# Two banded layers on one core: in every fourth step GpSimd's group-norm pass for the next step moves ahead of the inverse square roots

## The chip, the cores and the metric

The kernel runs on one core of a Trainium2 chip. The metric is device time in microseconds, from one launch to its end; the median of three runs is 5162.48 us (5158.28 to 5162.59). The profile is one execution of 5160.82 us, whose instructions span 5158.9 us. The five engines are called as the profile calls them: PE (TensorE, matmuls and transposes), DVE (VectorE), ACT (ScalarE), POOL (GpSimd) and SP (SyncE, which here only issues transfers).

## The reference

An image `x` of 512 x 512 places with 64 channels goes twice through the same layer, each with its own weights:

```python
v = group_norm(x)                       # 32 groups of 2 channels, over the whole image
xn = layer_norm(v)                      # over the 64 channels of a place
left  = (xn @ Wl + bl) * mask * sigmoid(xn @ Wlg + blg)      # 64 -> 128
right = (xn @ Wr + br) * mask * sigmoid(xn @ Wrg + brg)
gate  = sigmoid(xn @ Wog + bog)
# each of 128 channels: out[i, k] = sum over |j - i| <= 4 of left[j, i] * right[j, k]
out = banded(left, right)
x = x + (layer_norm(out) * gate) @ Wo + bo
```

The mean and the variance of the group norm need the whole image, so layer 2 cannot begin its main work before layer 1 has ended. All arithmetic is float32.

## The kernel before

**Tiling.** A unit is a tile `z` of 128 x 8 x 64: 64 rows of the image, 8 columns, taken once from the left half and once from the right half of the image (two halves on 128 partitions). Sixteen units (`NU`) make a chunk of 128 columns; a layer has 9 row blocks of two chunks, that is 18 chunks or 288 units. Work runs in **steps** `t`, one unit per step; below, a step's place in its chunk is written t mod 16.

**What one unit goes through**, in four to twenty steps: `load` (two transfers of 128 KB, issued on SP two steps before use), `affine` (the group norm: `z * ga`, then `z + gb`, two POOL operations in place), `inner_stats` (layer-norm statistics on DVE, one step after `affine`), `solve` (the inverse square roots for some four units at once, every fourth step), `inner_norm` (`z - mean`, then `z * rs`, two POOL operations in place), `transposed` (four PE transposes, copied by ACT to `zT`), `right` (the projections on PE, a sigmoid on ACT to `sg`, the product on DVE into `RO`). When a chunk's `right` is complete, `mix` multiplies it with the banded `left` in the next chunk's steps, on PE (`banks<-RO,A`). Those matmuls fall in the places t mod 16 = 0 to 9 only; the places 10 to 15 have none.

**What one output goes through**: `out_stats` on DVE (`sto`), the same `solve`, `norm` on ACT (`on<-RO,nm,rs`), `gates` and `turned` on PE, a product on DVE (`ZH`), the projection back on PE, `biased` on POOL (adds the bias to the tile `XR` that holds the old image), a sum on DVE (`end`) and the store by SP. Outputs trail units by 30 steps. In places 10 and 11 `out_stats` is done for two outputs per step, in places 8 and 9 for none, else for one.

**Order.** Every engine gets its instructions in the order in which the step loop of `layer` writes them (the wrapper `en` keeps program order, which is why nearly all lines of the profile say L362). Within one step POOL gets:

```python
for u in affines.get(t, []):
    affine(u, en.vector if u.at < NU + 4 else en.gpsimd)   # z<-z,ga ; z<-z,gb
...
for u in inputs(t + 2):
    inner_norm(u)                                          # z<-z,sti ; z<-z,rs
...
    biased(outs[t], w, stats)                              # XR<-XR,pack (or fewer)
...
if t % 4 == 3:
    solve(w, us, os, st, so)    # DVE: 5 small; POOL: 10 rsqrt/rs, then rs and nm
```

`solve` at step T serves the units T+3 to T+6. The first of them meets `inner_norm` in step T+1, and its transposes stand in step T+2 on PE. The inverse roots and means of the outputs are first used by `norm` in step T+2. DVE's share of `solve` comes last in its step: it ends with `rs<-var`, the first guess of the root, on which POOL's `rsqrt<-rs` waits. `affines` is planned ahead by the list `count = [1, 1, 2, 1, 1, 1, 2, 1, 1, 1, 1, 0, 1, 1, 1, 0]`: so many units get `affine` in a step of that place, some 8 steps before they are transposed. Buffers: `z` has 12, the roots `rs` 3, the banks of PSUM (`bank`) 3 in layer 1 and 4 in layer 2.

Of the kernel before, what the change touches and what calls it, by code (L numbers as in the profile page):

```python
# [24 lines left out]
NU = JC // JU  # L25
# [22 lines left out]
def mid(v: bass.AP, n: int) -> bass.AP:  # L48

    p, c = v.shape  # L50
    return v.unsqueeze(1).broadcast_to([p, n, c])
# [28 lines left out]
def tile_two_banded_layers(  # L80
# [298 lines left out]
    def load(src: bass.AP, u: Unit):  # L379
        u.z = zp.tile([P, JU, D], F32, tag="z", name="z")  # L380
        if u.near is None:
            rows = slice(u.blk.s, u.blk.s + S)
            for e, j in enumerate((u.j, LH + u.j)):
                en.sync.dma_start(u.z[e * S : (e + 1) * S], src[rows, j : j + JU, :])
            return
        spans = [(0, u.near, u.near + JU)]
        if u.near + JU > NEAR * JQ:
            spans = [(o, u.near, u.near + JQ) for o in range(0, JU, JQ)]
        for o0, n0, n1 in spans:
            for o, r, k, m in runs(n0, n1):  # L390
                z = u.z[:, o0 + o : o0 + o + m, :].rearrange("q m c -> q (m c)")
                at, q0, q1 = r * (L + 1) + k - WIN, 0, P
                pieces = []

                if r == 0 and k < WIN:
                    q0, g = 1, min(m, WIN - k)
                    pieces = [(0, 0, g, 0), (0, g, m, at + g)]
                if r == JQ - 1 and k + m > WIN + 1:
                    q1, g = P - 1, max(0, WIN + 1 - k)
                    end = (P - 1) * JQ * (L + 1) + at  # L400
                    pieces = [(P - 1, 0, g, end), (P - 1, g, m, L * L - m)]
                en.sync.dma_start(
                    z[q0:q1],
                    strided(
                        src, (q0 * JQ * (L + 1) + at) * D, (JQ * (L + 1) * D, q1 - q0), (1, m * D)
                    ),
                )
                for q, g0, g1, a in pieces:
                    if g0 < g1:
                        en.sync.dma_start(  # L410
                            z[q : q + 1, g0 * D : g1 * D],
                            strided(src, a * D, (D, 1), (1, (g1 - g0) * D)),
                        )

    def affine(u: Unit, engine):

        engine.tensor_tensor(u.z, u.z, mid(ga, JU), ALU.mult)
        engine.tensor_tensor(u.z, u.z, mid(gb, JU), ALU.add)
# [171 lines left out]
    def recall(o: Out):  # L590
        o.t = ztg.tile([P, JU // 2, P], F32, tag="zg", name="zg")
        en.sync.dma_start(o.t, later[o.at])
# [81 lines left out]
    def layer(src: bass.AP, dst: bass.AP, w: dict, stats: bool, then=None):  # L674
        per = LH // JC
        n_chunks = len(blocks) * per
        LAG = NU + 14
        own = NU - JW // JU
        units, outs, lefts, mixes, looks, slabs = {}, {}, {}, {}, {}, {}
        free = NA * [NU - 2]  # L680
        for c in range(n_chunks):
            b, t0 = blocks[c // per], (c + 1) * NU
            for k in range(NU):
                t = c * NU + k
                units[t] = u = Unit(t, blk=b, j=c % per * JC + k * JU)
                j = k * JU if c % 2 == 0 else (JC + k * JU if k < own else JC - JW + (k - own) * JU)
                u.c = j

            for f in range(NU):
                o = outs[c * NU + LAG + f] = Out(  # L690
                    b, units[c * NU + (f + own) % NU], c % per * JC + f * JU
                )
                looks.setdefault(t0 + (8 + f if f > 3 else 10 + f // 2), []).append(o)

            step = [t0 + n for n, k in enumerate((2, 1, 2, 2, 1, 2, 1, 2, 2, 1)) for _ in range(k)]
            for n, t in enumerate(step):
                mixes.setdefault(t, []).append((c, n * HB))

            for h in range(H // HA):
                slabs.setdefault(free[-NA], []).append((c, h))  # L700
                free.append(step[(h + 1) * (HA // HB) - 1] + 1)
        for n in range(0, NEAR * JQ, JU):
            t = 3 + n // JU * 2
            lefts[t] = Unit(t, near=n)
        first_t, last_t = min(outs), max(outs)

        def inputs(t: int) -> list:
            return [d[t] for d in (units, lefts) if t in d]

        loads, affines, inners = {}, {}, {}
        count = [1, 1, 2, 1, 1, 1, 2, 1, 1, 1, 1, 0, 1, 1, 1, 0]
        ahead = {}
        done = -5 - NU
        for t in range(-7 - NU, n_chunks * NU):
            for _ in range(count[t % NU]):
                ahead[done + 7] = t
                done += 1
        for t in range(n_chunks * NU):  # L720
            for u in inputs(t):
                loads.setdefault(ahead[t] - 2, []).append(u)
                affines.setdefault(ahead[t], []).append(u)
                inners.setdefault(ahead[t] + 1, []).append((t, u))

        early = [u for t in sorted(loads) for u in loads[t] if u.near is None and u.at < 7]
        for u in early:
            load(src, u)
        yield
        A, sti, sto = {}, {}, None  # L730
        for t in range(min(loads), last_t + 3):
            if then and t == max(units) + 2:
                then()
            for u in loads.get(t, []):
                if u not in early:
                    load(src, u)
            if t + 2 in outs:
                recall(outs[t + 2])
            if t + 1 in outs:
                fetch(src, outs[t + 1], w, t + 1)  # L740
            for c, h in slabs.get(t, []):
                A[c, h] = take_left(c // per, h)

            for o in looks.get(t, []):
                if sto is None:
                    sto = sm.tile([P, NB // 2, 6], F32, tag="sto", name="sto"), []
                st, os = sto
                for k in range(JU // 2):
                    out_stats(o, st[:, len(os) * (JU // 2) :], k)
                os.append(o)  # L750
            for u in affines.get(t, []):
                affine(u, en.vector if u.at < NU + 4 else en.gpsimd)
            if t in outs:
                gates(outs[t], w)

            todo = []
            for at, u in inners.get(t, []):
                key = (at + 2) // 4
                if key not in sti:
                    sti[key] = sm.tile([P, 3 * NB // 4, 6], F32, tag="sti", name="sti", bufs=3), []  # L760
                st, us = sti[key]
                n = len(us) * (JU // 2)
                u.mean = st[:, n : n + JU // 2, 1::3]
                todo += [(u, st[:, n : n + JU // 2, :], k) for k in range(JU // 2)]
                us.append(u)
            for v in todo[: len(todo) // 2]:
                inner_stats(*v)
            if t in units:
                for q in range(0, JU, JQ):
                    right(units[t], q, w)  # L770
            if t in lefts:
                for q in range(0, min(JU, NEAR * JQ - lefts[t].near), JQ):
                    left(lefts[t], q, w)
            for u in inputs(t + 2):
                inner_norm(u)
            for u in inputs(t + 1):
                transposed(u)
            if t in outs:
                turned(outs[t], w)
                biased(outs[t], w, stats)  # L780
            for v in todo[len(todo) // 2 :]:
                inner_stats(*v)
            if t - 1 in outs:
                end(dst, outs[t - 1], w)
            if stats and t - 2 in outs:
                sums(outs[t - 2], t - 2 == first_t, t - 2 == last_t)
            if t % 4 == 3:
                st, us = sti.pop((t + 5) // 4, (None, []))
                so, os = sto or (None, [])
                sto = None  # L790
                if us or os:
                    solve(w, us, os, st, so)
            if t + 1 in outs:
                norm(outs[t + 1])
            for n, (c, h0) in enumerate(mixes.get(t, [])):
                mix(c, A[c, h0 // HA], h0, [True, n + 1 < len(mixes[t])])
# [129 lines left out]
```

## Time and profile before

| | |
|---|---|
| median of three runs | 5162.48 us (5158.28 to 5162.59) |
| profiled execution | 5160.82 us, span 5158.9 us |
| PE busy | 4536.4 us, 88% |
| POOL busy | 3821.0 us, 74% |
| ACT busy | 3793.4 us, 74% |
| DVE busy | 3656.7 us, 71% |
| mean DMA rate | 190 GB/s |
| granted PE clock, mean | 0.97 of full speed |
| POOL `z<-z,ga` and `z<-z,gb` | 536 each, 1280 and 1278 ns |
| POOL `z<-z,sti` and `z<-z,rs` | 586 each, 1064 and 1054 ns |

A busy share is an average over stages: the first 300 us collect the statistics of the input, both layers ramp up and down, and between is a steady part that repeats with each chunk. What the change is worth is read in the steady part, from what each engine waits for there. The steady part of layer 1 reaches in this profile from about 560 to 2470 us, that of layer 2 from about 3050 to 4880 us.

### The profile page before, as it was taken

The page shows a single profiled execution, that of the slowest core. Times are in us where ns is not written, and L with a number is a line of the kernel's source. Part 1 is how long each engine was busy: PE and PEld are TensorE (multiplying, and loading weights), DVE is VectorE, ACT ScalarE, POOL GpSimd, SP SyncE. Part 2 cuts the span into 40 slices and gives each one's busy share as a digit, 9 for nine tenths or more (in the row PEclk, how much of TensorE's full clock was granted, in tenths as well). Part 3 has the DMA queues.
Part 4 walks back from the last instruction along what each step waited for, and adds up shares of the span by engine and source line. Part 5 has one row for each costly group of instructions (what it writes and reads, how often), then busy time and mean ns, then how long its engine had stood idle before and what let it go on. Part 6 is the DMA issues. An engine that isn't in the chain of part 4 may idle for free.

```text
span 5158.9 us, 159784 instructions
## 1 busy us (share of the span) xinstructions
PE 4536.4 (88%) x60138; PEld 3756.4 (73%) x60138; DVE 3656.7 (71%) x9445; ACT 3793.4 (74%) x8328; POOL 3821.0 (74%) x4739
## 2 busy tenths in 40 slices
PE   1037999999999999999995599999999999999999
PEld 0025788888888888888873378888888887888886
DVE  6864677777777777777766467777777777777776
ACT  0013788888888888888884268888888888888888
POOL 0037888888888888888733588888888888888863
PEclk9988999999999999999998799999999999999999
DMA  7924666666666666666663457667677776667766
GB/s 318 387 62 127 176 190 191 190 192 190 193 190 190 190 191 190 191 192 192 187 169 108 105 172 200 196 197 200 194 200 199 199 199 195 194 199 200 200 186 172
DMA packets 905291, 981.45 MB, mean 190 GB/s; under 512 B 114210, under 2 KB 641608, under 8 KB 900168
## 3 DMA queue, kind: packets, MB, share of 16 engines
q1 hardware_dynamic: 897248, 948.49, 63.6%
q10 hardware_dynamic: 7272, 22.73, 1.1%
q8 instruction: 477, 7.82, 0.7%
q14 instruction: 294, 2.41, 0.2%
HBM read 658.42 MB, written 312.46 MB: 188 GB/s over the span
## 4 chain that ended last, share of the span: by engine, by line
PE 73%; POOL 9%; DMA 5%; DVE 5%; ACT 3%; issue 2%; SPq 2%; another core or an unknown queue 0%; ACTq 0%; POOLq 0%; DVEq 0%
PE banks L362 37%; PE bank L362 34%; POOL z L362 5%; POOL rsqrt L362 2%; DMA left_of<-nothing 2%; ACT on L362 2%; PE acc L362 2%; SPq L362 2%; DVE RO L362 1%; DVE ZH L362 1%; DMA gn_x<-in_x_dram 1%; POOL rs L362 1%; DMA z<-mid_x 1%; ACT gate L362 1%; DVE sti L362 0%
## 5 line engine op out<-in xcount | busy, mean ns | idle before, releaser
L362 ACT ACTIVATE on<-RO,nm,rs 128x128 f32<-128x128 f32 x4608 | 1878.3, 494 | 183.9 <-PE bank L362 178.3
L362 PE MATMUL banks<-pack,zT 64*128 64x256 f32 x9360 | 1219.7, 389 | 133.9 <-ACT zT L362 79.3
L362 PEld LDWEIGHTS banks<-pack,zT 64*128 64x128 f32 x9360 | 974.4, 193 | 413.6 <-issue 172.7
L362 PE MATMUL banks<-RO,A 64*64 64x128 f32 x18432 | 1154.6, 277 | 0.0
L362 PEld LDWEIGHTS banks<-RO,A 64*64 64x64 f32 x18432 | 1082.4, 183 | 26.7 <-issue 3.3
L362 ACT ACTIVATE sg<-banks 128x512 f32<-128x512 f32 (+1 forms) x1188 | 684.0, 589 | 323.4 <-PE banks L362 207.0
L362 DVE TENSOR_TENSOR RO<-banks,sg 128x512 f32<-128x512 f32 x1152 | 748.8, 682 | 231.0 <-ACT sg L362 230.1
L362 DVE COPY RO<-banks 128x512 f32<-128x512 f32 x360 | 249.0, 692 | 930.6 <-ACT RO L362 930.6
L362 DVE SCALAR_TENSOR_TENSOR ZH<-bank,pack,gate 128x448 f32<-128x448 f32 (+1 forms) x1152 | 742.6, 684 | 99.2 <-PE bank L362 61.4
L362 DVE BATCH_NORM_STATS2 sto<-RO 128x6 f32<-128x256 f32 x2304 | 797.8, 412 | 1.2
L362 POOL TENSOR_TENSOR z<-z,gb 128x512 f32<-128x512 f32 x536 | 685.2, 1278 | 42.0
L362 POOL TENSOR_TENSOR z<-z,ga 128x512 f32<-128x512 f32 x536 | 685.8, 1280 | 0.1
L362 PE MATMUL bank<-zg,pack 64*128 64x448 f32 (+1 forms) x2304 | 665.5, 597 | 18.6 <-DVE ZH L362 16.3
L362 PE MATMUL bank<-pack,ZH 128*64 128x64 f32 x18432 | 677.9, 228 | 3.0 <-ACT zT L362 0.5
L362 PEld LDWEIGHTS bank<-pack,ZH 128*64 128x64 f32 x18432 | 597.9, 140 | 103.6 <-ACT zT L362 76.7
L362 ACT ACTIVATE gate<-bank 128x448 f32<-128x448 f32 (+1 forms) x1152 | 566.5, 542 | 128.8 <-PE bank L362 127.9
L362 POOL TENSOR_TENSOR z<-z,rs 128x512 f32<-128x512 f32 x586 | 617.7, 1054 | 46.0
L362 PE MATMUL bank<-ident,on 128*128 128x128 f32 x4608 | 632.3, 279 | 14.7 <-ACT gate L362 12.1
L362 POOL TENSOR_TENSOR z<-z,sti 128x512 f32<-128x512 f32 x586 | 623.4, 1064 | 0.0
L362 ACT COPY RO<-banks 128x512 f32<-128x512 f32 x792 | 440.1, 585 | 225.7 <-PE banks L362 224.6
L362 DVE BATCH_NORM_STATS2 sti<-z 128x6 f32<-128x128 f32 x2344 | 549.0, 283 | 66.6 <-POOL z L362 66.6
L362 PEld LDWEIGHTS bank<-ident,on 128*128 128x128 f32 x4608 | 532.9, 144 | 73.9 <-ACT on L362 24.2
(137 smaller groups left out, 3725.3 us busy)
## 6 DMA issues: line engine op xcount, KB each, us to landing
later<-zT SPq DMA_DIRECT2D x576, 256.0 KB
A<-left_of SPq DMA_DIRECT2D x576, 256.0 KB
zg<-later SPq DMA_DIRECT2D x576, 256.0 KB
z<-in_x_dram SPq DMA_DIRECT2D x576, 128.0 KB
z<-mid_x SPq DMA_DIRECT2D x576, 128.0 KB
gn_x<-in_x_dram SPq DMA_DIRECT2D x16, 4096.0 KB
XR<-in_x_dram SPq DMA_DIRECT2D x448, 112.0 KB
mid_x<-XR SPq DMA_DIRECT2D x448, 112.0 KB
```

The source lines that it names most:

```text
L362: return lambda *a, **k: tc.keep_in_program_order(f(*a, **k))
```

## The change

In the steps with t mod 4 = 3 (from t = 19 on) the units due for `affine` in the next step are taken out of the plan and get it in this step, on POOL, just before `solve`. Nothing is added or left out.

```diff
-        A, sti, sto = {}, {}, None
+        A, sti, sto, then_affine = {}, {}, None, []
...
-            for u in affines.get(t, []):
+
+            for u in affines.pop(t, []):
                 affine(u, en.vector if u.at < NU + 4 else en.gpsimd)
+            if t % 4 == 3 and t > NU:
+                then_affine = affines.pop(t + 1, [])
             if t in outs:
                 gates(outs[t], w)
...
                 so, os = sto or (None, [])
                 sto = None
+                for u in then_affine:
+                    affine(u, en.gpsimd)
+                then_affine = []
                 if us or os:
                     solve(w, us, os, st, so)
```

## The prediction

> **What bounds the kernel now.** I read the page's chain first, because busy shares alone (PE 88%, the others 71 to 74%) do not say who waits.
>
> ```profile
> PE 73%; POOL 9%; DMA 5%; DVE 5%; ACT 3%; issue 2%; SPq 2%; another core or an unknown queue 0%; ACTq 0%; POOLq 0%; DVEq 0%
> ```
>
> PE carries the end, but 9% of the chain is POOL. Then I asked the table of waits who holds PE up, in the steady part of layer 1 (668 to 2470 us) and of layer 2 (3150 to 4880 us); columns: total us, times, longest.
>
> ```profile
> PE bank L362 <- POOL z L362: 38.3, 15, 2.6
> PE bank L362 <- DVE ZH L362: 8.9, 14, 0.6
> ...
> PE bank L362 <- POOL z L362: 53.7, 17, 3.5
> PE bank L362 <- DVE ZH L362: 4.0, 16, 0.3
> ```
>
> The reader is to see that PE is never out of work for long except for `z` from POOL, fifteen times per layer: once per chunk. The PE timeline gives the places: every 128.2 us in layer 1 (668.58 to 2463.27 us in 14 intervals), every 123.1 us in layer 2 (3152.59 to 4875.60). One of each follows, first on PE, then on POOL (start, duration, instruction, and in brackets the idle time before it).
>
> ```profile
> 1561.05 1.89 PE L362 MATMUL banks<-pack,zT 64*128 64x256 f32 x16
> 1565.49 0.66 PE L362 MATMUL bank<-ident,z 128*128 128x128 f32 x4 [2.55 <-POOL z L362]
> ```
>
> ```profile
> 1548.68 1.19 POOL L362 TENSOR_TENSOR XR<-XR,fewer 120x512 f32<-120x512 f32 x1 [2.04 <-PE bank L362]
> 1556.16 0.29 POOL L362 TENSOR_TENSOR rsqrt<-rs 128x64 f32<-128x64 f32 x1 [6.29 <-DVE rs L362]
> ...
> 1560.68 1.27 POOL L362 TENSOR_TENSOR z<-z,ga 128x512 f32<-128x512 f32 x1
> 1562.03 1.27 POOL L362 TENSOR_TENSOR z<-z,gb 128x512 f32<-128x512 f32 x1
> 1563.26 1.06 POOL L362 TENSOR_TENSOR z<-z,sti 128x512 f32<-128x512 f32 x1
> 1564.39 1.04 POOL L362 TENSOR_TENSOR z<-z,rs 128x512 f32<-128x512 f32 x1
> ```
>
> This is the solve at place 11. Places 10 to 15 have no mix matmuls, so PE's steps are short there; DVE has two outputs' statistics in each of places 10 and 11, so its share of the solve comes late. POOL idles 6.29 us for it, does the roots (4.5 us), then an `affine` that nobody needs yet (2.58 us, from 1560.68 to 1563.26), and only then the `inner_norm` that PE waits for.
>
> Last, the granted clock, in the stretches that follow stalls at 1436.85, 1565.49 and 3890.99 us, and a later one (the column before the DMA share is PEclk).
>
> ```profile
> 1436.80:1441.00 4.20, 4.15 (x50) 3.82 (x52) 1.77 (x4) 2.23 (x6) 4.12 (x4) 0.59 0.18 66
> 1565.40:1569.60 4.20, 4.11 (x68) 3.49 (x70) 2.98 (x8) 3.06 (x8) 4.12 (x5) 1.00 0.19 66
> 3890.90:3895.10 4.20, 4.11 (x45) 3.71 (x45) 1.77 (x4) 2.23 (x6) 4.12 (x5) 0.59 0.18 68
> 3895.10:3903.00 7.90, 7.90 (x89) 6.01 (x85) 7.34 (x20) 7.56 (x20) 7.67 (x8) 1.00 0.52 149
> ```
>
> A stall costs more than its idle time when PE resumes at about half clock: all fifteen of layer 2 (3.5 us idle) do, and eight of the fifteen of layer 1 (2.55 us idle).
>
> **What the Trainium skill says.** "TensorE: Matmul & The Clock Gate", section "What's actually happening": the clock falls to half after an idle window of about 3.4 us, the window runs freely. The trace agrees on layer 2 (3.51 us idle, 0.59 granted) but shows the drop after 2.55 us in half of layer 1's stalls too, where the page asks for a whole idle window; I use the trace. The same page, section "Architectural detail: the array is 16× 32×32, not 1× 128×128": GpSimd's queue is strictly first in, first out. The trace agrees: at 1549.9 us `z<-z,ga` could have run, and POOL idled in front of `rsqrt`. "GPSIMD Engine Reference", section "8. Key points": it contends with VectorE when the latter reads two inputs from SBUF. DVE's eight `sto` statistics took 2.71 us with POOL busy (at 1542.60) and 2.70 us with POOL idle (at 1548.98): no contention here.
>
> **The change part by part.**
>
> *What moves.* By the loop and its `count` list, 65 units per layer, 130 in all: 260 POOL operations pass in front of the 12 operations of their solve. No DVE, ACT, PE or SP instruction changes its place, and nothing is added: POOL's work is the same.
>
> *Place 11, layer 1.* POOL is free at 1549.87 us (1548.68 + 1.19). Its 2.58 us end by 1552.5 us, inside the idle 6.29 us, so `rsqrt` still starts at 1556.16. `inner_norm` then starts at 1560.7 and ends 2.58 us earlier, at 1562.86 instead of 1565.44 us. PE was free at 1565.49 - 2.55 = 1562.94 us. The whole stall goes: 15 x 2.55 = **38.3 us**. What is late next? POOL's own cadence in places 12 to 14 (two `affine` operations, two `inner_norm`, `XR`, 5.87 us a step, as between 1565.39 and 1571.27) moves forward as a whole by the same 2.58 us, so it does not take the gain back. DVE had 1.44 us idle for the same `z` and 1.60 us behind it; its product into `RO` will wait for ACT's sigmoid instead (ends 1563.84), some 0.6 us later than a plain shift, which an idle 1.14 us at 1571.74 takes up.
>
> *Clock, layer 1.* A stall at full clock gives an interval of 127.46 us (1309.39 to 1436.85), one at half clock 128.64 (1436.85 to 1565.49). Without the stall no window has reason to fall: 8 x 1.18 = **9.4 us**.
>
> *Place 11, layer 2.* The same arithmetic at 3890.99 us: POOL idle 6.34 us before `rsqrt`, the `affine` from 3886.19 to 3888.77. `z` is ready at 3888.37 instead of 3890.95, PE free at 3887.48: 0.93 us of stall remain, too short for a drop. Before, the half clock made that PE step 6.79 us (3890.99 to 3897.78) instead of 5.22, so PE fell behind POOL; after, POOL sets the next two steps (5.87 us each). Following both queues: `z` transposes at 3888.4, 3894.3, 3900.1, then 3905.4 us, against 3890.99, 3897.78, 3903.00, 3908.63 before. Gain 2.9 to 3.2 us a chunk; ACT's order (5.9 us a step) gives the same 3.2. I take 3.1: 15 x 3.1 = **46.5 us**. From below 2.58 (clock gives nothing), from above 4.2 (all of the 1.57 us too).
>
> *The ramps.* Steps before t = 19 keep the old order. The first solve at place 11 in each layer stalls PE by 5.31 us (at 541.56) and 4.12 us (at 3031.16), with POOL idle 5.04 and 4.02 us before it: 2.6 us each, part of the clock perhaps: **5.5 us**. After 4880 us no unit is left.
>
> *The other solves* (places 15, 3, 7). POOL idles 0.7 to 1.7, 2.2 to 2.7 and 3.9 us there in layer 1, and 0.7 to 2.4 us in layer 2 (steady part). Where that is less than 2.58 us, `rsqrt` starts up to 1.9 us later, but `inner_norm` never later: the sum of POOL's work ahead of it is the same. PE does not wait there, so I cost them at nothing. What covers the late roots is that `norm` uses them in step T+2, over a step of some 8 us away; without that cover up to 1.9 us per solve would fall on ACT.
>
> *The new wait.* `z<-z,ga` waits for its transfers, and behind it now stand `rsqrt`, the next `inner_norm` and PE. The loads are issued at the same place as before (1540.68 to 1541.80 us for the unit of 1560.68), some 8 us before POOL can reach them. In layer 2 the pair issued at 3866.55 is followed in SP's queue by the `XR` pair at 3868.33, and POOL used that `XR` at 3874.13 without waiting for a transfer; the moved `affine` starts at 3875.3. Landing is not shown by itself; from below the cost is nothing, from above what the third rival says. I take nothing.
>
> *Sum*: 38.3 + 9.4 + 46.5 + 5.5 = 99.7 us. The profiled execution has 5160.8 us, so 5061; the median of the runs shown lies 1.7 us above it: **5063 us**.
>
> **The rivals.**
>
> 1. *Half is given back.* After the stall ACT (5.9 us a step), POOL (5.87) and PE (5.2 to 5.9) run neck and neck in places 12 to 15. If ACT, whose idle 2.34 us before `zT` at 1566.18 disappears, holds PE by 1.3 us per chunk, and the clock still falls at times, some 30 x 1.3 + 10 us are lost: about 5112 us. For it: the small margins. Against it: ACT's copy is only some 0.2 us later than a plain shift, and PE needs it a step later.
> 2. *No change.* The `z` of the moved pass lands only when POOL's wait for DVE ends, so the idle time cannot be used: 5162 us. Against it: the `XR` evidence.
> 3. *Slower: the load holds the roots.* Place: the first operation of the moved `affine`, before the solve at place 11. It decides once `z` lands later than 1556.16 - 2.58 = 1553.6 us, 11.8 us after its issue; break-even is landing at 1556.1, 14.3 us after. At 2 us beyond that, PE waits 2 us longer in 32 chunks: 5162 + 64 = 5226 us. In the ramp POOL once waited 10.8 us for a `z` transfer; in the steady part never.
>
> That the reordering is not made is excluded by the loop: the units are popped from the plan and nothing else issues them.
>
> **How the numbers follow.** A measurement of this kernel can tell some 0.2%, 10 us, from no change. The main case gets 0.76 (its own range 5042 to 5083: all of the half-clock time gained, or 2.58 us per stall alone), the half gain 0.17, no change 0.02, slower 0.05. The range takes in the main case and most of the half gain: 5042 to 5104. Faster 0.93, same 0.02, slower 0.05.
>
> **What would show it.** After: the wait of PE for `z` from POOL near nothing in layer 1 and about 1 us in three places per chunk in layer 2; POOL's idle time before `rsqrt` at place 11 smaller by 2.6 us; `z<-z,gb` directly before `rsqrt<-rs`; a clock of 1.00 through both steady parts; chunks of about 125 and 120 us. I am wrong if `z<-z,ga` shows idle time ended by a transfer, if the wait before `zT` or `RO` grows into a wait of PE, or if chunks shorten by less than 2 us.

## The result, and the profile after

The changed kernel takes 5071.39 us (median; 5070.62 to 5074.14) beside 5161.35 us for the kernel before: a ratio of 0.9828, 95% interval 0.9811 to 0.9845. It is faster by 90 us where 99.7 were forecast. The profiled execution has 5074.14 us and a span of 5072.3 us, 86.6 less than before. One execution of the run e1 below took 14999.2 us at a granted clock of 0.35, and the ratios leave it out.

PE's waits in the steady part of layer 2 (3050 to 4860 us), then of layer 1 (640 to 2440 us); columns: total us, times, longest:

```profile
PE bank L362 <- POOL z L362: 31.6, 45, 1.0
PE banks L362 <- DVE RO L362: 14.1, 11, 1.4
PE bank L362 <- DVE ZH L362: 4.0, 15, 0.3
...
PE bank L362 <- DVE ZH L362: 9.5, 15, 0.6
PE banks L362 <- DVE RO L362: 1.4, 5, 0.3
```

In layer 1 the wait for `z` is gone. In layer 2 three short ones per chunk stand in place of each long one: 0.95, 0.59 and 0.58 us at 3098.00, 3103.88 and 3109.75 us. The prediction had 0.93 for the first, and its steps of 5.87 us on POOL beside 5.22 on PE leave 0.65 for each of the others. The second line is new: eleven times PE now waits some 1.28 us for `RO`. POOL at place 11 of layer 1 after the change (start, duration, instruction, idle time before it):

```profile
1397.09 1.18 POOL L362 TENSOR_TENSOR XR<-XR,fewer 120x512 f32<-120x512 f32 x1 [3.01 <-PE acc L362]
1398.24 1.28 POOL L362 TENSOR_TENSOR z<-z,ga 128x512 f32<-128x512 f32 x1
1399.59 1.27 POOL L362 TENSOR_TENSOR z<-z,gb 128x512 f32<-128x512 f32 x1
1406.21 0.29 POOL L362 TENSOR_TENSOR rsqrt<-rs 128x64 f32<-128x64 f32 x1 [5.34 <-DVE rs L362]
...
1410.74 1.05 POOL L362 TENSOR_TENSOR z<-z,sti 128x512 f32<-128x512 f32 x1
```

The pass fills a part of the idle time, 5.34 us of it are left, and `inner_norm` follows the roots at once. The granted clock (the column before the DMA share) over 34 us of layer 1 and over the 4.2 us after a wait of layer 2:

```profile
1406.00:1440.00 34.00, 33.72 (x475) 27.70 (x471) 28.29 (x68) 30.84 (x71) 31.36 (x46) 1.00 0.68 204
...
3098.00:3102.20 4.20, 4.20 (x56) 3.53 (x58) 4.20 (x10) 3.50 (x9) 4.12 (x4) 1.00 0.53 177
```

It is full in both, as everywhere in the steady parts. A chunk takes 125.1 us in layer 1 and 120.8 in layer 2 (means of 14), beside 128.2 and 123.1 before.

**Where the missing microseconds went.** The profile has a number that the prediction had not asked about: DVE is busy for 3732.8 us instead of 3656.7, with the same 9445 instructions. The groups of DVE show which: the solve's small operations `var<-sti`, `var<-sto,pack`, `var<-var` and `nm<-sto` went from means of 249, 193, 181 and 176 ns to 396, 314, 399 and 280 ns. One solve at place 15 of layer 2, first DVE, then POOL, then PE at the start of the mix:

```profile
3113.48 0.69 DVE L362 TENSOR_SCALAR var<-sti 128x32 f32<-128x32 f32 x1
3114.09 1.32 DVE L362 SCALAR_TENSOR_TENSOR var<-sto,pack 128x32 f32<-128x32 f32 x1
3115.44 0.18 DVE L362 TENSOR_SCALAR var<-var 128x32 f32<-128x32 f32 x1
3115.53 1.27 DVE L362 TENSOR_SCALAR nm<-sto 128x32 f32<-128x32 f32 x1
3116.72 0.18 DVE L362 TENSOR_SCALAR rs<-var 128x64 int32<-128x64 int32 x1
```

```profile
3112.93 1.19 POOL L362 TENSOR_TENSOR XR<-XR,pack 120x512 f32<-120x512 f32 x1
3114.07 1.28 POOL L362 TENSOR_TENSOR z<-z,ga 128x512 f32<-128x512 f32 x1
3115.44 1.32 POOL L362 TENSOR_TENSOR z<-z,gb 128x512 f32<-128x512 f32 x1
```

```profile
3118.87 0.39 PE L362 MATMUL banks<-RO,A 64*64 64x128 f32 x2 [1.28 <-DVE RO L362]
```

Read the ends: `var<-sti` ends at 3114.17 and POOL's `XR` at 3114.12; `var<-sto,pack` at 3115.41 and `z<-z,ga` at 3115.35; `nm<-sto` at 3116.80 and `z<-z,gb` at 3116.76. Each long DVE operation ends just after the POOL operation beside it. This is the rule and not one case: from 560 us on, 121 of these operations (with `rs<-var`) took over 0.45 us in the changed kernel, 18 in the kernel before, and every one of them ended 0.03 to 0.06 us after a POOL instruction. The five in the solve shown take 3.4 us, from 3113.48 to 3116.90; behind them in DVE's order, without idle time, stand the last products into `RO`, which the mix needs.

In the kernel before, a solve at place 15 of layer 2 takes 1.2 us on DVE (3168.07 to 3169.29). First DVE, then POOL:

```profile
3168.07 0.65 DVE L362 TENSOR_SCALAR var<-sti 128x32 f32<-128x32 f32 x1
3168.65 0.19 DVE L362 SCALAR_TENSOR_TENSOR var<-sto,pack 128x32 f32<-128x32 f32 x1
...
3168.97 0.17 DVE L362 TENSOR_SCALAR nm<-sto 128x32 f32<-128x32 f32 x1
```

```profile
3167.51 1.18 POOL L362 TENSOR_TENSOR XR<-XR,pack 120x512 f32<-120x512 f32 x1
3169.37 0.29 POOL L362 TENSOR_TENSOR rsqrt<-rs 128x64 f32<-128x64 f32 x1 [0.68 <-DVE rs L362]
```

POOL stands still beside all but the first, because it waits for the last of these very operations. The first shows that the warning was in the trace before the change: `var<-sti` runs beside `XR`, takes 0.65 us where it takes 0.18 beside an idle POOL (3090.43 us in the changed kernel), and ends with `XR`. Place 11 escapes: there POOL has finished the pass long before. In layer 1 the five operations grow too, from 54.5 to 85.8 us in all from 640 to 2440 us, but PE waits for `RO` for 1.4 us only; what covers them there, and in the four chunks of layer 2 without the wait, was not followed.

### The profile page after: what moved, and what is told of

It reads as the page before. It is cut to its first block, busy times and chain, and to the rows that moved or that the text cites. A ratio compares the mean times of both kernels' runs of the same rounds, so it can differ in the third digit from the quotient of the medians.

```text
span 5072.3 us, 159784 instructions
## 1 busy us (share of the span) xinstructions
PE 4496.1 (89%) x60138; PEld 3714.8 (73%) x60138; DVE 3732.8 (74%) x9445; ACT 3793.8 (75%) x8328; POOL 3826.9 (75%) x4739
## 4 chain that ended last, share of the span: by engine, by line
PE 72%; POOL 9%; DMA 6%; DVE 4%; ACT 3%; issue 2%; SPq 2%; another core or an unknown queue 0%; ACTq 0%; POOLq 0%; DVEq 0%
PE banks L362 38%; PE bank L362 32%; POOL z L362 6%; ACT on L362 2%; DMA left_of<-nothing 2%; PE acc L362 2%; SPq L362 2%; DVE RO L362 1%; POOL XR L362 1%; DMA gn_x<-in_x_dram 1%; POOL rsqrt L362 1%; DVE ZH L362 1%; DMA XR<-mid_x 1%; DVE sto L362 1%; ACT gate L362 1%
## 5 line engine op out<-in xcount | busy, mean ns | idle before, releaser
L362 DVE SCALAR_TENSOR_TENSOR ZH<-bank,pack,gate 128x448 f32<-128x448 f32 (+1 forms) x1152 | 740.0, 682 | 37.6 <-ACT gate L362 36.3
L362 PE MATMUL bank<-pack,ZH 128*64 128x64 f32 x18432 | 663.5, 225 | 2.8 <-ACT zT L362 0.3
L362 PEld LDWEIGHTS bank<-pack,ZH 128*64 128x64 f32 x18432 | 584.0, 138 | 100.3 <-ACT zT L362 83.2
L362 PE MATMUL bank<-ident,on 128*128 128x128 f32 x4608 | 616.6, 274 | 14.7 <-ACT gate L362 12.1
L362 PEld LDWEIGHTS bank<-ident,on 128*128 128x128 f32 x4608 | 519.7, 141 | 74.0 <-ACT on L362 24.3
L362 POOL TENSOR_TENSOR XR<-XR,pack 120x512 f32<-120x512 f32 (+1 forms) x352 | 418.4, 1189 | 192.4 <-DMA XR<-mid_x 90.4
```

The costliest lines, as they stand in the source:

```text
L362: return lambda *a, **k: tc.keep_in_program_order(f(*a, **k))
```

## The experiments

| run | median us | ratio to before, 95% interval |
|---|---|---|
| changed kernel | 5071.39 | 0.9828 (0.9811 to 0.9845) |
| e1: place 11 only | 5058.77 | 0.9803 (0.9783 to 0.9822) |
| e2: places 15, 3, 7 only | 5175.02 | 1.0025 (1.0015 to 1.0035) |
| e3: moved pass in quarters | 5062.90 | 0.9833 (0.9796 to 0.9871) |
| e4: half of the pass, place 11 | 5105.23 | 0.9895 (0.9880 to 0.9910) |
| e5: e1 with a late load | 5080.30 | 0.9844 (0.9827 to 0.9860) |
| e6: e1, output scales later | 5049.78 | 0.9787 (0.9772 to 0.9802) |
| e7: e1, two units ahead | 5045.86 | 0.9781 (0.9766 to 0.9795) |
| e8: e6 and e7 together | 5037.10 | 0.9763 (0.9748 to 0.9777) |

**e1: only the solve at place 11 keeps the pass ahead of it.**

```diff
-            if t % 4 == 3 and t > NU:
+            if t % NU == 11 and t > NU:
                 then_affine = affines.pop(t + 1, [])
```

> The pass is moved ahead of the solve at place 11 only; at places 15, 3 and 7 it stays where it was. Theory (the gain is all from place 11, and the moved pass at the other places runs beside DVE's small operations of the solve and lengthens them, which holds PE up at place 0 of 11 chunks of layer 2 by some 1.28 us): PE's waits for RO in front of the mix go, chunks of layer 2 shorten from 120.9 to about 120.0 us, DVE's small operations (var, nm) return to the means of the kernel before (181 to 249 ns instead of 280 to 399), about 5058 us (5054 to 5063). Rival (the moves at the other three places carry part of the gain): slower than the changed kernel's 5071, up to 5100 us.

Measured 5058.77 us, and in the steady part of layer 2 PE has only these waits left:

```profile
PE bank L362 <- POOL z L362: 31.4, 45, 1.0
PE bank L362 <- DVE ZH L362: 4.4, 18, 0.3
```

The wait for `RO` is gone, chunks of layer 2 take 119.9 us, and the three middle operations are back at 189, 181 and 175 ns (`var<-sti` is still at 337: at place 15 it starts while POOL's `XR` runs). So one place out of four carries the whole gain of 103 us, and the other three cost 12.6 (the difference of the two medians).

**e2: the other three places, without place 11.**

```diff
-            if t % 4 == 3 and t > NU:
+            if t % 4 == 3 and t % NU != 11 and t > NU:
```

> The pass is moved ahead of the solve at places 15, 3 and 7 only; at place 11 it stays behind the roots. Theory: PE's fifteen stalls per layer for z return at 2.55 and 3.5 us with their half clock; DVE's small operations are as long as in the changed kernel (means of 280 to 399 ns), but the stall at place 11 gives DVE the slack that hides it: about 5162 us (5155 to 5180). Rival (the gain comes from GpSimd's earlier work at any solve): three quarters of it remain, about 5094 us.

5175.02 us, slower than before by a quarter of a per cent, with an interval clear of 1. In layer 2:

```profile
PE bank L362 <- POOL z L362: 49.2, 14, 3.5
PE banks L362 <- DVE RO L362: 6.8, 10, 0.7
```

The stalls are back in full and the wait for `RO` stays, at 0.7 us instead of 1.3. I had expected DVE's operations as long as in the changed kernel and the stall's slack to hide them. Neither came out: the means of `var<-sto,pack` and `nm<-sto` are 228 and 189 ns, near those of the kernel before, and in the solve behind the wait at 3424.93 the five take 2.6 us (3420.40 to 3422.97) instead of 3.4. There `var<-sti` starts 0.3 us after `z<-z,ga` and not 0.6 us before it, and one operation fewer is held to the end of a POOL instruction. The time lies 13 us above the 5162 that I had put first; the waits for `RO` are 7.7 us of that (both layers), the rest was not followed. The rival of 5094 us is out.

**e3: each moved operation in four pieces of 128 elements.**

```diff
                 for u in then_affine:
-                    affine(u, en.gpsimd)
+                    for k in range(4):
+                        v = u.z[:, 2 * k : 2 * k + 2, :]
+                        en.gpsimd.tensor_tensor(v, v, mid(ga, 2), ALU.mult)
+                    ...                            # the same with gb, ALU.add
```

> As the changed kernel, but each moved operation of 512 elements per partition is issued as four of 128 (eight instead of two instructions per unit). Theory (a small DVE operation waits until the GpSimd instruction in progress has ended): no small DVE operation is longer than some 0.6 us, the means of var and nm fall towards 250 ns, PE's wait of 1.28 us at place 0 falls below 0.6 us or goes, about 5062 us (5055 to 5070); place 11 is not hurt, since GpSimd has over 5 us idle there. Rival (the two engines share bandwidth, whatever the length of an instruction): the small operations stay as long as they are and the wait of 1.28 us stays, 5071 us or more.

5062.90 us (three of the four executions took 5061.41 to 5063.80 us, one 5104.45, which makes the interval wide and stays unexplained). The same solve at place 15, on DVE:

```profile
3112.69 0.69 DVE L362 TENSOR_SCALAR var<-sti 128x32 f32<-128x32 f32 x1
3113.30 0.19 DVE L362 SCALAR_TENSOR_TENSOR var<-sto,pack 128x32 f32<-128x32 f32 x1
3113.52 0.31 DVE L362 TENSOR_SCALAR var<-var 128x32 f32<-128x32 f32 x1
3113.75 0.17 DVE L362 TENSOR_SCALAR nm<-sto 128x32 f32<-128x32 f32 x1
3113.86 0.42 DVE L362 TENSOR_SCALAR rs<-var 128x64 int32<-128x64 int32 x1
```

Behind `XR`, which is still one long operation, nothing is longer than 0.42 us here (0.51 is the most that `var<-sto,pack` and `nm<-sto` reach in the run), and PE's waits for `RO` fall from 14.1 to 2.1 us, although POOL has more to do (1.78 us for the four `ga` pieces instead of 1.28). That the length of one POOL instruction bounds the delay is so supported. The expected means were missed: they are 347, 315, 275 and 295 ns, `rs<-var` has grown as well, and the total of the five groups is the 240 us of the changed kernel, against 153 before. The waits are shorter but more solves have them; what the two engines share, and by which rule, these runs do not settle.

**e4: only `z * ga` ahead, at place 11.** It asks what the length of the stall is worth.

```diff
                 for u in then_affine:
-                    affine(u, en.gpsimd)
+                    en.gpsimd.tensor_tensor(u.z, u.z, mid(ga, JU), ALU.mult)
+                halves = then_affine               # z + gb: first on POOL in the next step
```

> At place 11 only, and only the first of the pass's two operations (z times ga) is moved ahead of the solve; the second stays behind the roots. PE's stall should be 1.29 us shorter: about 1.27 us in layer 1, 2.2 us in layer 2. Theory (a long stall also costs half-clock time): no half clock follows the 1.27 us, so layer 1 gains 15 x 1.29 + 9.4 = 28.8 us; layer 2 gains 15 x 1.3 = 19.5 us if the half clock stays, 30 us if it goes; with 2.6 us in the ramps 5100 to 5111 us in all, chunks of layer 1 all equally long. Rival (the clock has no part): 33 x 1.29 = 42 us gained, 5119 us, with the half clock still in every second chunk of layer 1.

5105.23 us. The stalls are 1.20 us in layer 1 and 2.17 us in layer 2. Clock after two stalls of layer 2 and one of layer 1:

```profile
3122.90:3127.10 4.20, 4.19 (x56) 3.53 (x58) 3.06 (x8) 3.14 (x8) 4.12 (x4) 1.00 0.27 82
3243.90:3248.10 4.20, 4.16 (x46) 3.76 (x46) 1.78 (x5) 1.87 (x5) 4.12 (x4) 0.59 0.36 115
793.70:797.90 4.20, 4.15 (x68) 3.53 (x70) 3.61 (x9) 3.10 (x8) 4.12 (x4) 1.00 0.28 90
```

No stall of 1.20 us is followed by half clock, nine of the fifteen of 2.17 us are. Chunks of layer 1 take 126.15 us (128.19 before): 2.0 us shorter for a stall that is 1.35 us shorter. The half clock is a price of its own; the rival's 5119 us lies outside the run's 5101.28 to 5107.52.

The length of the stall alone does not decide, though: 2.17 us are followed by half clock in nine of fifteen cases, 2.55 us before the change in eight of fifteen. And one stall of 3.51 us, the first in the steady part of layer 2 of the kernel before, is followed by full clock:

```profile
3152.50:3156.70 4.20, 4.11 (x56) 3.45 (x58) 2.98 (x8) 3.06 (x8) 4.12 (x5) 1.00 0.17 64
```

In the steady parts the granted clock changes only at times that are whole multiples of 3.413 us apart: in the kernel before half clock begins at 1437.34 and at 1693.34 us, 75 such intervals later. I cut PE's 90 long waits for `z` in the steady parts of three traces (before, e2, e4) at these times. Where at least 2.02 us of the wait lie inside one interval, half clock follows at that interval's end (55 cases); where at most 1.97 us do, it does not (35 cases). The wait that ends at 1436.85 lies whole in one interval. The one that ends at 1565.49 is cut into 0.69 and 1.85 us, and the clock stays full. A chunk of layer 1 is 37.6 intervals long, so the cut falls elsewhere in each chunk. The stall of the line above is cut into twice 1.75 us.

**e5: the load of the moved unit one step later, to bring about the prediction's slower rival.**

```diff
-                loads.setdefault(ahead[t] - 2, []).append(u)
+                late = ahead[t] % NU == 12 and ahead[t] > NU
+                loads.setdefault(ahead[t] - 2 + late, []).append(u)
```

> As e1_only11, but the transfers of the unit that is passed ahead at place 11 are issued one step later, at the start of place 11 instead of place 10, some 6 us before DVE's part of the solve ends instead of some 14 us. This is the prediction's slower rival, made to happen. Theory: an XR transfer landed within some 4.6 us of its issue here, so z lands some 1.5 to 1.9 us too late for the pass to be over when rsqrt could start; rsqrt waits that long in 32 chunks: about 5110 us (5080 to 5140), with a wait of z<-z,ga for a DMA in the trace. Rival (transfers land in 2 us): as e1_only11, 5058 us.

5080.30 us, 21.5 more than e1, at the low edge of what was expected. POOL:

```profile
3100.54 1.27 POOL L362 TENSOR_TENSOR z<-z,ga 128x512 f32<-128x512 f32 x1 [4.30 <-DMA z<-mid_x]
3101.89 1.28 POOL L362 TENSOR_TENSOR z<-z,gb 128x512 f32<-128x512 f32 x1
3103.84 0.29 POOL L362 TENSOR_TENSOR rsqrt<-rs 128x64 f32<-128x64 f32 x1 [0.67 <-DVE rs L362]
```

The pass does wait for its transfer, but the roots do not wait for the pass: `z` had landed within 3.5 us of its issue at 3097.09, the pass ends at 3103.17, and `rsqrt` then still idles 0.67 us for DVE. In all 32 such solves the pass ends before DVE's `rs<-var`. So the slower rival was not made to happen. What costs here is again DVE beside POOL:

```profile
3102.47 0.74 DVE L362 TENSOR_SCALAR var<-sti 128x32 f32<-128x32 f32 x1
```

It ends at 3103.21, just after `z<-z,gb`, and the five operations take 1.3 us; over the 32 solves their mean is 1.32 us, and 0.73 in e1. That is 0.6 us in each, which would make 19 of the 21.5 us. With the load where the change left it, a step or some 9 us earlier, the rival had no chance.

**e6: the solve's last two POOL operations (`rs`, `nm` for outputs) behind the next `inner_norm`.**

```diff
-            en.gpsimd.tensor_tensor(ro, ro, w["m"][:, js], ALU.mult)
-            en.gpsimd.tensor_tensor(nm, nm, ro, ALU.mult)
+            def out_scales(): ...                  # these two, called after
+            rest.append(out_scales)                # inner_norm of step T+1
```

> As e1_only11, but the solve's last two GpSimd operations (rs and nm for the outputs, 0.6 us) stand behind the next step's inner_norm instead of ahead of it. Theory (behind the roots GpSimd's own cadence sets PE's steps at places 12 to 14 of layer 2): the first wait of PE for z falls from 0.95 to 0.35 us, the second grows by 0.6 us, nothing is gained: 5058 us (5055 to 5062). Rival (only the chain up to the first z counts): 15 x 0.6 = 9 us less, 5049 us.

5049.78 us, 9.0 less than e1: the rival's number. The trace does not follow the rival, though. PE at places 12 to 14 of one chunk of layer 2:

```profile
3091.28 0.66 PE L362 MATMUL bank<-ident,z 128*128 128x128 f32 x4 [0.30 <-POOL z L362]
...
3097.69 0.65 PE L362 MATMUL bank<-ident,z 128*128 128x128 f32 x4 [1.12 <-POOL z L362]
...
3103.56 0.66 PE L362 MATMUL bank<-ident,z 128*128 128x128 f32 x4 [0.58 <-POOL z L362]
```

The first wait shrank and the second grew, as my theory had it, and chunks shortened by 0.19 us in layer 2 and 0.13 in layer 1, some 5 us in all. The other 4 us lie outside the steady parts, 2.4 of them in the ramp of layer 2 (from its first transposes to its first chunk, 234.8 us in e1 and 232.4 here). Why that ramp shortened is open.

**e7: at place 11 the pass for two units.**

```diff
-                loads.setdefault(ahead[t] - 2, []).append(u)
+                early_load = ahead[t] % NU == 13 and ahead[t] > NU
+                loads.setdefault(ahead[t] - 2 - early_load, []).append(u)
...
-                then_affine = affines.pop(t + 1, [])
+                then_affine = affines.pop(t + 1, []) + affines.pop(t + 2, [])
```

> As e1_only11, but at place 11 the pass is done ahead of the solve for the units of both places 12 and 13 (the second one's transfers are issued a step earlier). GpSimd has 4.5 us idle there, so the roots start on time; places 12 and 13 then have no pass to do. Theory (ACT, 5.87 us a step, is as full as GpSimd): PE's second and third waits for z in layer 2 (0.59 and 0.58 us) go, but ACT's sigmoid and so RO come no earlier, and PE waits about 0.9 us for RO at place 0: 5055 us (5052 to 5059). Rival (GpSimd alone held these steps): 15 x 1.17 = 17 us less, 5041 us.

5045.86 us, 12.9 less than e1, between the two and nearer to the rival. The second and third wait for `z` are gone, and no wait of PE for `RO` over 0.3 us has come in their place. ACT shows why my theory failed:

```profile
3095.86 3.25 ACT L362 ACTIVATE on<-RO,nm,rs 128x128 f32<-128x128 f32 x8 [0.35 <-PE bank L362]
...
3101.29 3.24 ACT L362 ACTIVATE on<-RO,nm,rs 128x128 f32<-128x128 f32 x8
...
3106.71 3.27 ACT L362 ACTIVATE on<-RO,nm,rs 128x128 f32<-128x128 f32 x8
```

ACT's 5.87 us a step had held a pause of 0.35 us for PE's transposes. With PE earlier the pause goes, and ACT runs at 5.42 us a step (3101.29 to 3106.71): the limit lay there, not at 5.87. Chunks of layer 2 take 119.3 us.

**e8: e6 and e7 together.**

```diff
+            rest.append(out_scales)                # as in e6
...
+                then_affine = affines.pop(t + 1, []) + affines.pop(t + 2, [])   # as in e7
```

> e6_defer and e7_two11 together, for the version that may beat both kernels. Theory (ACT holds places 12 to 15): as e7_two11, 5055 us (5050 to 5059). Rival (GpSimd alone held them): 15 x 1.77 = 27 us less than e1_only11, 5032 us.

5037.10 us, nearer to the rival again. In layer 2:

```profile
PE bank L362 <- DVE ZH L362: 4.5, 17, 0.3
PE bank L362 <- POOL z L362: 4.3, 15, 0.3
```

This version beats both kernels: 123 us less than before (5159.97 us, measured with it), 34 less than the change. It reads the same data and does the same operations, but only place 11 has the pass moved, for two units, with two small operations of the solve moved behind the next `inner_norm`.

## Why the prediction was right, and which term was off

The sum was 99.7 us against the profiled execution, and its span fell by 86.6. The mechanism held, and the shortfall has one cause, which e1 takes away. The stretches between the same instructions in the two traces split that:

- *Ramps*, 5.5 us predicted. The first `z` stall of layer 1 moves from 541.56 to 538.55 us (3.0), the ramp of layer 2 (from its first transposes, 2795.53 and 2745.80, to 3031.16 and 2979.14) shortens by 2.3: 5.3. Right.
- *Layer 1 with its clock*, 38.3 + 9.4 = 47.7 us. From that stall to the statistics between the layers (2766.92 and 2717.15) it is 2225.4 before and 2178.6 after: 46.8. Right, and e4 supports that the clock is a term of its own. One reading was wrong: of the fifteen stalls of layer 2 fourteen are followed by half clock, not all. And why eight of layer 1's are, the prediction left open; e4 answers it. Neither changes the sum by much.
- *Layer 2*, 46.5 us. From 3031.16 and 2979.14 to the end: 2127.7 and 2093.2, a gain of 34.6. **This is the term that was off, by 12 us.** The steps inside it held (the three waits near their predicted sizes, the clock at 1.00), but eleven new waits of PE for `RO`, 14.1 us together, came on top. With the pass at place 11 only (e1) the same stretch, from 2978.20 us to the end, takes 2079.0 us: a gain of 48.7 beside the 46.5 predicted. A sign that the prediction had named for being wrong, the wait for `RO` growing into a wait of PE, is what came, in layer 2.
- *The step that failed* is the pair "no contention here" and "The other solves [...] I cost them at nothing". I had looked at one kind of DVE operation, the `sto` statistics, which indeed take the same with POOL busy (412 and 411 ns on average in the two kernels), and had carried that over to all of DVE. "GPSIMD Engine Reference", section "8. Key points", names instructions with two SBUF inputs and those in a two-port mode; the prediction gave the first half only, and tested it on statistics that read one input. `var<-sto,pack` reads two inputs from SBUF and was over six times as long in the solve shown (1.32 against 0.20 us), so there the page and the trace agree. `nm<-sto` reads one and was as long (1.27 us); that it ran in a two-port mode, no run here shows. Before the change POOL stood still beside nearly all of these operations, and I named as cover for POOL's work the very time in which DVE needed POOL to be still. At place 11 the pass of 2.6 us ends before them; at place 15 POOL's idle time was 0.7 to 1.7 us in layer 1 and 1.1 us in most of layer 2, so it cannot.
- *The new wait on the load* cost nothing, as taken: in the steady part of layer 2 POOL waits in front of `rsqrt<-rs` and of `XR` only. In e5, with the load a step later, the roots still waited for DVE and never for the pass, so what a later landing would cost was not measured.
- *Rival 1* had a give-back of about this size per chunk (1.3 us), but by ACT and in all chunks. ACT was not the cause, and e7 shows that it had 0.4 us a step to spare; the cause was DVE beside POOL, in layer 2.

## What to carry to other kernels

Work put into another engine's idle time is free only if that engine's idleness was not needed: ask what ran beside the gap, operation by operation, and compare its durations with and without a neighbour; the trace before the change can already hold both. Move a piece of work only at the one stage where the wait ends last; here one place of four carried all of the gain, and moving it elsewhere too cost an eighth of it. When an engine seems full, look for the pauses inside its step before calling its step its limit.

## What the runs showed of the hardware

- DVE operations of 0.2 us on SBUF took up to 1.3 us while POOL ran two-input operations of 1.28 us, and ended within 0.06 us of them; with POOL's operations cut to quarters, `var<-sto,pack` and `nm<-sto` took up to 0.51 us. Statistics (`sto<-RO`) stayed at 411 to 412 ns on average in every run.
- PE's idle times were followed by half clock: those of 3.5 us in 14 of 15 cases, 2.55 us in 8 of 15, 2.17 us in 9 of 15, 1.20 us in none of 15. What decided all of them was how much fell inside one of the intervals of 3.413 us at whose ends the clock changed: 2.02 us or more, half clock; 1.97 us or less, full clock (90 cases, worked out under e4). "TensorE: Matmul & The Clock Gate", section "What's actually happening", asks for an idle window of about 3.4 us; these runs show the drop after less.
- A pair of 128 KB loads landed within 3.5 us of the first one's issue (e5, 3097.09 to 3100.54 us), with the DMA engines 65% busy.
